# One matmul moved behind a block product in a gated graph network's step, and a score copy taken to where the scores are made

## The chip, the cores and the metric

The kernel runs on one core of a Trainium2 chip. The metric is the device time of one execution in microseconds (us), from the first to the last instruction of the program; the lower, the better. TensorE (PE in the profile, with its weight loads as PEld), VectorE (DVE), ScalarE (ACT), GpSimd (POOL) and SyncE (SP, DMA issues only) each run their own list of instructions in order, and wait for each other by semaphores.

## The reference, cut to what matters

The input is 64 graphs of 256 nodes with 256 features each (`x`, 64x256x256, float32) and an adjacency matrix per graph (`adj`, int32). Two layers follow each other, both with a layer norm and a relu ahead of them and a residual sum behind:

```python
# layer 0: three steps of a gated graph network (w_ih, w_hh are shared, weight[i] is the step's own)
h0 = relu(layernorm(x)); h = h0
for i in range(3):
    aggr = A^T @ (h @ weight[i])          # A = (adj != 0), per graph
    gi, gh = aggr @ w_ih.T + b_ih, h @ w_hh.T + b_hh
    r = sigmoid(gi_r + gh_r); z = sigmoid(gi_z + gh_z)
    n = tanh(gi_n + r * gh_n)
    h = (1 - z) * n + z * h
x = x + h
# layer 1: graph attention with 4 heads of 64
h = relu(layernorm(x)) @ W.T + b
logits = leaky_relu(l_src[i] + l_dst[j], 0.2), barred where adj is not 1
x = x + softmax(logits over j) @ h
```

`l_src` and `l_dst` are the two scores of each node and head, made from `h` and the vectors `a`.

## The kernel before, in words

**Tiling.** Graphs are taken in 32 pairs. The state of a pair lies transposed in one tile `hT_a` (128 partitions, two halves of the features, 2 x 256 nodes). `weight[i]` and `w_ih` are multiplied into one matrix `w_a` per step beforehand, so that a step multiplies the aggregated state `aggr` and the state `hT_a` by 256x256 weight blocks. For the r and z gates, and again for the state's part of n, the eight block products of a two-by-two block multiplication are brought down to seven by sums and differences of blocks (the tiles `T1` to `T4`, `T2n` to `T4n` and the weight blocks `S1` to `S4`, `NS1` to `NS4`); that is why partial results such as `m5`, `m5n`, `pd` and `pe` go from one bank of PSUM to another.

**Order.** The schedule is written out by hand. `plan` holds, for each tick, three lists: STEP (the gated step), READY (work for VectorE, ScalarE and GpSimd whose inputs are there) and REST (the rest, mainly TensorE work that fills in). The lists of a tick are issued in that order, and every engine runs what it was given in that order. A pair starts 18 ticks after the one before; a gated step takes six ticks (`tick_0` to `tick_5`) and a pair has three, at ticks 0, 12 and 24, so the steps of neighbouring pairs alternate and there is always exactly one step under way. The attention of a pair (values at ticks 37 and 38, score rows at 39, maxima, logits, exponentials, and the output products at 62 to 65) lies in the READY and REST lists of the ticks in which later pairs make their steps.

**Banks.** A step takes its banks of PSUM from a ring of five (`gate_bank`): `qa`, `qb`, `pc`, `p5` (called `p` in the profile), `pd`, `pe`, `pn0`, `pn1`. Everything else takes banks from a ring of three (`bank`).

**Around the change, first place.** `tick_0` makes n's first product (weight `N00`) in the left half of bank `qa`; ScalarE copies it to `qb` (L411). Then come the 16 aggregation matmuls in two banks `pa`, each copied to `aggr` by ScalarE (L422), and at the end the product `NS1` x `T1` in the right half of the same bank `qa`, which ScalarE copies to `m5n` (L424). `tick_1` began with n's second product (`N01`), accumulated onto the left half of `qa`; ScalarE turns that half into `hn` with the bias (`state_n`, L399). Then come `NS2` x `T2n` onto `qb`, a sum on VectorE (L433), the block product of the state for the r gate into `pc` (four matmuls in the program, eight in the profile), and the copy of `pc` to `pd` on ScalarE (L437). All matmuls of the step have float32 operands; the profile shows each as two. `part` (L396) issues the small products and `block` (L293) the block products.

**Second place.** `values` makes the four blocks of values and scores of a pair, two at tick 37 and two at tick 38: two matmuls for each into `pv`, and a sum with the bias on VectorE into `val` (L605). A row of `val` holds 4 x 65 values and then 8 scores. `score_rows`, at tick 39, copied the scores of all four blocks to a tile `score` (L636 on VectorE), and `as_rows` transposes it on TensorE (`pscore`, L615), copies the result out (L617) and sends it to DRAM, from where it is read back on all partitions. For the last pair the score rows are made per graph, at ticks 37 and 38.

Of the kernel before, what the change touches and what calls it, by code (L numbers as in the profile page):

```python
# [9 lines left out]
F32 = mybir.dt.float32  # L10
# [7 lines left out]
P = 128  # L18
# [8 lines left out]
def gated_gnn_then_gat_kernel(  # L27
# [39 lines left out]
    nc = tc.nc  # L67
    B, N, D = x.shape
    L = weight.shape[0]
    H, C2 = a.shape  # L70
# [5 lines left out]
    R = PB * KN  # L76
    T = PB * N
    VC = C + 1
    S0 = H * VC
# [7 lines left out]
    small = ctx.enter_context(tc.tile_pool(name="small", bufs=4))  # L87
# [9 lines left out]
    def bank(name):  # L97
        return ps_m.tile([P, 512], F32, tag="mm", name=name)
# [5 lines left out]
    def buf(tag, shape, name, dtype=F32):  # L104
        return sb.tile(shape, dtype, tag=tag, name=name, bufs=BUFS.get(tag, 1))
# [86 lines left out]
    N00, N01, N11, NS1, NS2, NS3, NS4 = range(7)  # L192
# [90 lines left out]
    def flat(y):  # L283
        return y.rearrange("q r d -> q (r d)")
# [4 lines left out]
    def block(pt, w, j, src, start=False):  # L289

        for c in range(KD):
            for k in range(KD):
                nc.tensor.matmul(  # L293
                    pt[:, ts(c, N)], w[:, k, j * D + c * P : j * D + (c + 1) * P], src[:, k, :],
                    start=start and c == 0 and k == 0, stop=(c == KD - 1 and k == KD - 1),
                    skip_group_check=True,
                )
# [64 lines left out]
    def of(y, i):  # L362
        return y[:, :, ts(i, N)]

    class Step:
# [60 lines left out]
        def tick_1(self):  # L426
            h0 = of(self.hT(), 0)
            q_a, q_b = self.qa, self.qb
            self.own("hn", [P, KD, T])
            self.part(q_a[:, :N], N01, h0[:, 1, :])  # L430
            self.state_n(0, 0, q_a[:, :N])
            self.part(q_b[:, :N], NS2, self.T2n)
            nc.vector.tensor_add(q_b[:, N:], q_b[:, :N], self.m5n)  # L433
            p_c = self.bank("pc")
            block(p_c, w_h, RH, h0, start=True)
            self.bank("p5")
            nc.scalar.copy(self.bank("pd"), p_c)  # L437
            T3 = self.own("T3", [P, KD, N])
            nc.vector.tensor_sub(T3, of(self.aggr, 1), of(self.hT(), 1))
            nc.vector.tensor_add(self.own("T2", [P, KD, N]), T3, h0)  # L440
# [64 lines left out]
    def plan_pair(p):  # L505
        t0 = APART * p
        v = {}
# [84 lines left out]
        blocks_of = {u: slice(u.start * KN, u.stop * KN) for u in units}  # L592

        def values(r0):
            def fn():
                if r0 == 0:
                    v["val"] = buf("val", [P, R, VW], f"val_{p}")
                for r in (r0, r0 + 1):
                    pt = bank(f"pv_{p}_{r}")
                    for k in range(KD):  # L600
                        nc.tensor.matmul(  # L601
                            pt[:, :VW], hb["hT"][:, k, ts(r, P)], w_val[:, k, :],
                            start=(k == 0), stop=(k == KD - 1),
                        )
                    nc.vector.tensor_add(v["val"][:, r, :], pt[:, :VW], b_val)  # L605
            return fn

        rest(37, values(0))
        rest(38, values(2))

        def as_rows(src, n, what, u):

            m = len(u) * KN * n
            pt = bank(f"p{what}_{p}_{u.start}")
            nc.tensor.transpose(pt[:m, :P], flat(src), ident)  # L615
            fl = buf("flat", [m, P], f"{what}_{p}_{u.start}")
            nc.vector.tensor_copy(fl, pt[:m, :P])  # L617
            rows = dram.tile([len(u), n, N], F32, tag=f"{what}{len(u)}", name=f"{what}_dram_{p}_{u.start}")
            for y in range(len(u)):
                for s in range(KN):  # L620
                    nc.sync.dma_start(rows[y, :, ts(s, P)], fl[(y * KN + s) * n : (y * KN + s + 1) * n, :])
            return {i: rows[i - u.start] for i in u}

        def on_all(rows, h0, blocks):

            src = rows[h0 : h0 + H, :]
            return bass.AP(tensor=src.tensor, offset=src.offset, ap=[[0, P], [0, blocks], [1, H * N]])

        scores, tops, drow, mrow, logits, link = {}, {}, {}, {}, {}, {}

        def score_rows(u):
            def fn():
                if u.start == 0:
                    v["score"] = small.tile([P, R, 2 * H], F32, tag="score", name=f"score_{p}", bufs=2)
                sc = v["score"][:, blocks_of[u], :]
                nc.vector.tensor_copy(sc, v["val"][:, blocks_of[u], S0:])  # L636
                scores.update(as_rows(sc, 2 * H, "score", u))
                for i in u:
                    drow[i] = buf("row", [P, H, N], f"drow_{p}_{i}")
                    nc.sync.dma_start(drow[i].rearrange("q h n -> q (h n)"), on_all(scores[i], H, 1)[:, 0, :])  # L640
            return fn
# [170 lines left out]
```

## Time and profile before

| | before |
|---|---|
| median time of three runs | 2687.61 us (2687.0 to 2689.67) |
| span of the profiled execution | 2687.4 us |
| TensorE matmuls busy | 2564.9 us (95%) |
| TensorE weight loads busy | 2259.6 us (84%) |
| VectorE busy | 1853.6 us (69%) |
| ScalarE busy | 1466.7 us (55%) |
| GpSimd busy | 653.4 us (24%) |
| DMA, mean | 89 GB/s |

Busy time is the union of an engine's instructions in the profile. Matmuls are pipelined, so that their spans overlap: one of the step's matmuls lasts 379 ns in the profile, while in an unbroken row one starts every 216 ns. A gap on TensorE is therefore read from the starts of matmuls. The work repeats for each pair: in the middle of the run the same matmul comes back every 79.9 us. In the profile's views a line such as "L396" is the line of the kernel's text, and names such as `qa<-T,w_n` say which tile is written from which.

### The profile page before, as it was taken

The page shows a single profiled execution, that of the slowest core. Times are in us where ns is not written, and L with a number is a line of the kernel's source. Part 1 is how long each engine was busy: PE and PEld are TensorE (multiplying, and loading weights), DVE is VectorE, ACT ScalarE, POOL GpSimd, SP SyncE. Part 2 cuts the span into 40 slices and gives each one's busy share as a digit, 9 for nine tenths or more (in the row PEclk, how much of TensorE's full clock was granted, in tenths as well). Part 3 has the DMA queues.
Part 4 walks back from the last instruction along what each step waited for, and adds up shares of the span by engine and source line. Part 5 has one row for each costly group of instructions (what it writes and reads, how often), then busy time and mean ns, then how long its engine had stood idle before and what let it go on. Part 6 is the DMA issues. An engine that isn't in the chain of part 4 may idle for free.

```text
span 2687.4 us, 38787 instructions
## 1 busy us (share of the span) xinstructions
PE 2564.9 (95%) x14074; PEld 2259.6 (84%) x14074; DVE 1853.6 (69%) x4497; ACT 1466.7 (55%) x3077; POOL 653.4 (24%) x518
## 2 busy tenths in 40 slices
PE   7899999999999999999999999999999999999985
PEld 5688888888888888888888888888888888888875
DVE  4567766777766777776677776677776677776663
ACT  2345555655555555655565555555555565555553
POOL 0012222222222222322222322222222222222221
PEclk9899999999999999999999999999999999999995
DMA  2004344434344433334443334443434443333444
GB/s 86 18 9 99 83 103 95 111 79 87 82 100 97 108 85 87 87 89 105 100 97 84 89 82 107 95 109 81 87 79 103 95 111 81 86 89 85 95 95 110
DMA packets 120320, 239.89 MB, mean 89 GB/s; under 512 B 9792, under 2 KB 79424, under 8 KB 120128
## 3 DMA queue, kind: packets, MB, share of 16 engines
q0 software_dynamic: 34272, 132.13, 25.6%
q1 hardware_dynamic: 80160, 102.52, 12.5%
q10 hardware_dynamic: 5696, 2.76, 0.4%
q8 instruction: 111, 1.82, 0.3%
q14 instruction: 81, 0.66, 0.1%
HBM read 219.82 MB, written 17.56 MB: 88 GB/s over the span
## 4 chain that ended last, share of the span: by engine, by line
PE 88%; ACT 5%; DVE 4%; issue 1%; DMA 1%; POOL 0%; ACTq 0%; SPq 0%; DVEq 0%; POOLq 0%
PE pd L293 18%; PE pn L293 12%; PE pc L293 10%; PE po L750 9%; PE qb L396 6%; PE p L293 6%; PE pe L293 6%; PE pa L418 5%; PE pv L601 4%; PE qa L396 4%; PE pback L552 3%; ACT aggr L422 2%; ACT zz L662 1%; PE pt_a L351 1%; PE pt_b L351 1%
## 5 line engine op out<-in xcount | busy, mean ns | idle before, releaser
L487 POOL TENSOR_TENSOR R<-hT_a,hn 128x512 f32<-128x512 f32 x192 | 318.3, 1658 | 930.4 <-ACT hn L484 865.9
L293 PE MATMUL pn<-aggr,w_a 128*128 128x256 f32 x1536 | 367.0, 382 | 0.0
L293 PE MATMUL pd<-T,w_a 128*128 128x256 f32 x1536 | 364.6, 380 | 0.0
L293 PEld LDWEIGHTS pn<-aggr,w_a 128*128 128x128 f32 x1536 | 287.1, 190 | 42.9 <-DVE pn L473 6.2
L293 PEld LDWEIGHTS pd<-T,w_a 128*128 128x128 f32 x1536 | 286.8, 190 | 36.9
L750 PEld LDWEIGHTS po<-val,zz 128*128 128x128 f32 x2048 | 258.6, 201 | 16.7 <-ACT zz L741 12.0
L750 PE MATMUL po<-val,zz 128*128 128x65 f32 x2048 | 255.9, 281 | 11.1 <-ACT zz L741 11.1
L690 DVE CUSTOM_DVE_ANT_0 any<-drow,noedge 128x256 f32<-128x256 f32 x512 | 244.7, 478 | 15.2 <-DMA drow<-score_dram 6.2
L763 POOL TENSOR_TENSOR x<-x,o 128x256 f32<-128x256 f32 x128 | 117.3, 917 | 524.4 <-DVE o L758 524.4
L403 ACT ACTIVATE R<-pc,brz 128x256 f32<-128x256 f32 x192 | 80.5, 470 | 296.6 <-PE pc L293 296.6
L484 ACT ACTIVATE hn<-pn,bi 128x256 f32<-128x256 f32 x384 | 160.4, 470 | 144.5 <-PE pn L293 144.4
L718 ACT ACTIVATE zz<-zz,val 128x256 f32<-128x256 f32 x512 | 231.9, 509 | 8.4 <-DMA zz<-score_dram 8.4
L502 DVE SCALAR_TENSOR_TENSOR R<-Z,R 128x512 f32<-128x512 f32 x192 | 131.7, 686 | 147.3 <-POOL R L487 142.6
L558 DVE TENSOR_TENSOR hNlo<-pback,hNhi 128x512 fp32r<-128x512 f32 x128 | 88.5, 691 | 183.0 <-ACT hNhi L557 183.0
L403 ACT ACTIVATE R<-pe,brz 128x256 f32<-128x256 f32 x192 | 80.5, 470 | 215.3 <-PE pe L293 215.3
L503 DVE SCALAR_TENSOR_TENSOR hT_a<-R,hn 128x512 f32<-128x512 f32 x192 | 174.9, 911 | 13.3
L473 DVE SCALAR_TENSOR_TENSOR pn<-R,hn 128x512 f32<-128x512 f32 x192 | 142.8, 744 | 59.8 <-ACT R L403 31.6
L293 PE MATMUL pd<-T,w_h 128*128 128x256 f32 x768 | 181.4, 379 | 0.0
L293 PE MATMUL pc<-hT_a,w_h 128*128 128x256 f32 x768 | 181.4, 379 | 0.0
L293 PE MATMUL p<-T,w_a 128*128 128x256 f32 x768 | 181.4, 379 | 0.0
L293 PE MATMUL pc<-aggr,w_a 128*128 128x256 f32 x768 | 181.4, 379 | 0.0
L293 PE MATMUL pe<-aggr,w_a 128*128 128x256 f32 x768 | 181.4, 379 | 0.0
(147 smaller groups left out, 5304.6 us busy)
## 6 DMA issues: line engine op xcount, KB each, us to landing
zz<-score_dram POOLq DMA_DIRECT2D x64, 1024.0 KB, 12.1
zz<-topT_dram POOLq DMA_DIRECT2D x62, 1024.0 KB, 8.0
adj<-in_adj_dram SPq DMA_DIRECT2D x64, 512.0 KB
drow<-score_dram SPq DMA_DIRECT2D x64, 512.0 KB
x<-in_x_dram SPq DMA_DIRECT2D x32, 512.0 KB
out_dram<-x SPq DMA_DIRECT2D x32, 512.0 KB
score_dram<-score SPq DMA_DIRECT2D x128, 4.0 KB
topT_dram<-topT SPq DMA_DIRECT2D x128, 2.0 KB
```

What stands on the lines that cost most here:

```text
L293: nc.tensor.matmul(pt[:, ts(c, N)], w[:, k, j * D + c * P : j * D + (c + 1) * P], src[:, k, :], start=start and c == 0 and k == 0, stop=(c ...
L396: nc.tensor.matmul(pt, w_n[:, j, :], src, start=start, stop=True, skip_group_check=True)
L403: nc.scalar.activation(of(dst, i)[:, c, :], src[:, c, :], AF.Tanh, bias=brz[:, g0 + c : g0 + c + 1], scale=0.5)
L418: nc.tensor.matmul(pt[:, ts(i, N)], hN[half][:, i * KN + s, ts(e, P)], edge[:, i * KN + s, :], start=(s == 0 and half == 0), stop=(s == KN ...
L473: nc.vector.scalar_tensor_tensor(by_c(self.bank(f"pn{i}")), of(self.R, i), 1.0, of(self.hn, i), op0=ALU.add, op1=ALU.mult)
L484: nc.scalar.activation(n__[:, c, :], p_n[:, c, :], AF.Tanh, bias=bi[:, 2 * KD + c : 2 * KD + c + 1])
L487: nc.gpsimd.tensor_sub(of(self.R, i), of(self.hT(), i), n__)
L502: nc.vector.scalar_tensor_tensor(d_, of(self.Z, i), 1.0, d_, op0=ALU.add, op1=ALU.mult)
L503: nc.vector.scalar_tensor_tensor(of(self.hT(), i), d_, 0.5, of(self.hn, i), op0=ALU.mult, op1=ALU.add)
L690: nc.vector.tensor_tensor_reduce(any_, drow[r // KN][:, h, :], v["noedge"][:, r, :], 1.0, -3.0e38, ALU.add, ALU.max, accum_out=v["top"][:, ...
L718: nc.scalar.activation(zz[:, h, :], zz[:, h, :], AF.Prelu, alpha=ALPHA, bias=v["val"][:, r, S0 + H + h : S0 + H + h + 1],)
L750: nc.tensor.matmul(po[:, ts(h_, VC)], logits[i][:, j, h_, ts(s, P)], v["val"][:, i * KN + j, ts(h_, VC)], start=(j == 0), stop=(j == KN - 1),)
```

## The change

In `tick_1` n's second product and the activation that reads it go behind the block product `pc`, with `NS2` x `T2n` on `qb` now first. The purpose is to put other matmuls between `NS1`, whose result ScalarE takes out of bank `qa`, and the next matmul that writes this bank. In the second place the copy of the scores goes from `score_rows` into `values`: each two blocks are copied right behind the sums that make them, so that the transpose at tick 39 finds its input ready. The arithmetic stays the same.

```diff
             self.own("hn", [P, KD, T])
-            self.part(q_a[:, :N], N01, h0[:, 1, :])
-            self.state_n(0, 0, q_a[:, :N])
             self.part(q_b[:, :N], NS2, self.T2n)
             nc.vector.tensor_add(q_b[:, N:], q_b[:, :N], self.m5n)
             p_c = self.bank("pc")
             block(p_c, w_h, RH, h0, start=True)
+            self.part(q_a[:, :N], N01, h0[:, 1, :])
+            self.state_n(0, 0, q_a[:, :N])
             self.bank("p5")
             nc.scalar.copy(self.bank("pd"), p_c)
...
                     nc.vector.tensor_add(v["val"][:, r, :], pt[:, :VW], b_val)
+                if r0 == 0:
+                    v["score"] = small.tile([P, R, 2 * H], F32, tag="score", name=f"score_{p}", bufs=2)
+                nc.vector.tensor_copy(v["score"][:, r0 : r0 + 2, :], v["val"][:, r0 : r0 + 2, S0:])
...
         def score_rows(u):
             def fn():
-                if u.start == 0:
-                    v["score"] = small.tile([P, R, 2 * H], F32, tag="score", name=f"score_{p}", bufs=2)
-                sc = v["score"][:, blocks_of[u], :]
-                nc.vector.tensor_copy(sc, v["val"][:, blocks_of[u], S0:])
-                scores.update(as_rows(sc, 2 * H, "score", u))
+                scores.update(as_rows(v["score"][:, blocks_of[u], :], 2 * H, "score", u))
```

## The prediction

> **What bounds the kernel now.** I read the page's busy times first, then the chain that ended last, then TensorE's list of waits, and last the timeline around each of the two largest waits. Busy times and chain, from the page:
>
> ```profile
> PE 2564.9 (95%) x14074; PEld 2259.6 (84%) x14074; DVE 1853.6 (69%) x4497; ACT 1466.7 (55%) x3077; POOL 653.4 (24%) x518
> ...
> PE 88%; ACT 5%; DVE 4%; issue 1%; DMA 1%; POOL 0%; ACTq 0%; SPq 0%; DVEq 0%; POOLq 0%
> ```
>
> TensorE sets the time: 88% of the chain are its own instructions, and no other engine is over 69% busy. What can be won without taking matmuls away is the 9% of ScalarE and VectorE in the chain, where TensorE stood still for them. Who they are is in the list of waits, once for the matmuls and once for the weight loads (total us, times, longest):
>
> ```profile
> PE qa L396 <- ACT m5n L424: 35.9, 66, 0.6
> PE pscore L615 <- DVE score L636: 18.8, 33, 2.0
> ...
> PEld qa L396 <- ACT m5n L424: 62.4, 66, 1.0
> PEld pscore L615 <- PE pc L293: 26.4, 30, 0.9
> ```
>
> The two largest waits are exactly the two that the diff touches. A matmul's span in the profile is longer than its share of an unbroken row, so the 35.9 and 18.8 us are lower ends of the loss; the idle time of the weight loads, 62.4 and 26.4 us, counts time too in which the matmul before still ran, and is an upper end. The true loss is read from starts. The timeline of one step (start, length, engine, line, names):
>
> ```profile
> 1191.79 0.59 PE L396 MATMUL qa<-T,w_n 128*128 128x256 f32 x2
> 1191.99 0.58 ACT L422 COPY aggr<-pa 128x512 f32<-128x512 f32 x1 [0.37 <-PE pa L418]
> 1192.47 0.38 ACT L424 COPY m5n<-qa 128x256 f32<-128x256 f32 x1
> ...
> 1192.91 0.70 PE L396 MATMUL qa<-hT_a,w_n 128*128 128x256 f32 x2 [0.52 <-ACT m5n L424]
> ...
> 1193.44 0.59 PE L396 MATMUL qb<-T2n,w_n 128*128 128x256 f32 x2
> ```
>
> In an unbroken row these matmuls start every 216 ns (the eight of `pc` take 1.73 us in the chain). Four of them lie between 1191.79 and 1193.44, which should take 0.86 us and took 1.65: 0.79 us lost. ScalarE copies the second half of `aggr` first and then `m5n`, and n's second product waits for that, though it writes the other half of the bank. In the next pair's step, in the chain of waits:
>
> ```profile
> 1242.19 0.99 ACT aggr L422 x2
> 1243.19 0.28 ACT m5n L424
> 1243.47 0.04 issue
> 1243.51 0.70 PE qa L396 x2
> ```
>
> There the `NS1` product started at 1242.27 and the product onto `qb` at 1244.05: 1.78 - 0.86 = 0.92 us lost. These two kinds of step alternate with a third, in which `pt_b` and `plink` already stand between the two products; that one has almost no wait (0.05 us), which is why the list says 66 times for 96 steps. For the scores:
>
> ```profile
> 1228.08 1.89 PE L293 MATMUL pc<-aggr,w_a 128*128 128x256 f32 x8
> 1228.28 0.70 DVE L457 TENSOR_TENSOR pe<-pd,m 128x512 f32<-128x512 f32 x1 [0.55 <-PE pd L293]
> ...
> 1230.15 0.17 DVE L636 COPY score<-val 128x32 f32<-128x32 f32 x1
> ...
> 1230.47 0.27 PE L615 MATMUL pscore<-ident,score 128*32 128x128 f32 x1 [0.51 <-DVE score L636]
> ```
>
> The eight `pc` matmuls end their row at 1228.08 + 1.73 = 1229.81; the transpose starts at 1230.47, 0.66 us later. The copy itself is short (0.17 us); it came late because VectorE first made `pe` and the three state sums `T`, `T3n` and `T2n`.
>
> **What the Trainium skill says.** "Perfetto Trace Analysis", section "Optimization Strategy", says to find the gaps of the engine that binds, see what semaphore ends each, and make that start sooner; that is the reading above. "TensorE: Matmul & The Clock Gate", section "Part 2: What happens when you issue a matmul", says that matmuls stay in program order while weight loads are pulled ahead of running matmuls. The trace agrees: a weight load of 190 ns costs nothing in the rows of `pc` (one start every 216 ns), but shows as 0.1 us behind each stop, 0.53 instead of 0.43 us from 1192.91 to 1193.44. So a matmul that waits holds all behind it, and moving independent ones ahead is the remedy. "VectorE: DVE Perf Modes", section "The TRN2 errata", says that small operations pay a fixed cost per instruction; here a score copy of 32 columns takes 173 ns and one of 16 (the last pair's) 174 ns, so halving a copy makes it no cheaper.
>
> **The change part by part.**
>
> *N's second product behind `pc`.* No instruction is added. Behind the `NS1` product now follow two matmuls on `qb` (0.43 us) and eight on `pc` (1.73 us) before bank `qa` is written again, 2.16 us in all. `m5n` was there 1.06 and 1.20 us after the start of `NS1`, the next writer now comes 2.59 us after it: over 1.3 us of room. What comes first now must not wait either. The product on `qb` needs `T2n` and the copy to `qb` (L411); in the slowest kind of step that copy ended at 1242.19, and the product will start at 1242.70. `pc` takes the bank that `pe` of the step before left, which ScalarE read long ago. So 0.79 and 0.92 us go, 0.85 on average: 66 x 0.85 = 56.1 us. The third kind I count at nothing, since behind the bf16 `plink` the 0.1 us of weight load stays.
>
> *The activation behind `pc`.* On ScalarE `hn` from `qa` (L399) now waits until about 3.0 us after `NS1` starts, and the copy `pd` (L437) queues behind it, together with an exponential (L741) in one kind of step and a leaky relu (L718) in the other. In the second kind of step: products end at 1245.29, `hn` (0.48) and `pd` (0.57) are done near 1246.5, before 1246.98 until now; the exponential (1.06) near 1247.6, needed by `po` at 1249.67 - 0.92 = 1248.75. `pd` is wanted by TensorE at 1251.41 - 0.92 = 1250.5. In the first kind `pd` is done near 1195.95 and wanted at 1198.7. Cost: nothing, hidden by matmuls.
>
> *VectorE, which doesn't all move up with TensorE.* In the first kind of step it works from 1191.98 to 1201.14 almost without a gap, so part of it keeps its old time. The sum on `qb` (L433) ended at 1194.62, and `NS3` onto `qb` will want it at 1196.04 - 0.79 = 1195.25: 0.63 us of room, the tightest place. `pe` (L457) had 0.36 us of idle time ahead of it and will lag TensorE by 0.79 - 0.36 = 0.43 us, where 1.63 us of room were. Behind it, `pn` (L473) had only 0.07 us of room; but it hangs on ScalarE's row from the end of `pc` (gate, `hNhi_a`, leaky relu, `hT_a`, `hn`), ahead of which ScalarE sat idle 2.46 us. That row moves up as a whole. Cost: nothing.
>
> *The score copies.* 31 pairs: one copy of 173 ns is replaced by two of about 174, in the ticks before, 31 instructions and 5.4 us of VectorE more. The second lies in the 0.55 us that VectorE sat idle ahead of `pe`. The transpose then finds its input over 1 us before it comes. 31 x 0.66 = 20.5 us. In the last pair the rows are made right behind the values, and nothing moves.
>
> Sum: 56.1 + 20.5 = 76.6 us, so 2687.6 - 76.6 = 2611 us. TensorE's clock was granted in full (1.00) through the middle of the run and can't rise; stops of under 1 us were not costing clock.
>
> **The rivals.**
>
> *Half comes back as new waits.* For it: VectorE and ScalarE keep their old times in part of each step, and 0.63 us is little. Against it: every other place has over 0.8 us. If `NS3` or `po` waits 0.6 us in 66 steps, 39.6 us are lost: about 2651.
>
> *Another chain paces the step.* If the chain from `pn` through ScalarE, GpSimd and the state's update back to the next product were binding, the 56 us would come back whole and only the scores' 20.5 remain: 2667. Against it: TensorE waits for `hT_a` only twice (3.4 us in its list).
>
> *Slower.* If `pn`, with its 0.07 us, slipped by the length of the moved activation and the copy behind it (0.48 + 0.57 us) in all 96 steps, that is 101 us, over the 76.6 won: 2712. For it: in-order ScalarE. Against it: the 2.46 us of idle time between the moved work and that row.
>
> **How the numbers follow.** The forecast, 0.82; half back, 0.09; paced elsewhere, 0.05; slower, 0.03; a remainder of 0.01 for no change. Together: faster 0.96, within 0.2% 0.01, slower 0.03. Low end: the upper ends of the loss, 62.4 + 26.4 = 88.8 us, give 2599. High end: the lower ends, 35.9 + 18.8 = 54.7 us, give 2633; I put it at 2636, which holds the forecast with a few us of new waits.
>
> **What would show it.** In the changed profile: no row of `qa` waiting for `m5n`, none of `pscore` waiting for `score`; a pair's period of 79.9 - 0.79 - 0.92 - 0.66 = 77.5 us; ScalarE's and VectorE's share of the chain down from 9% to some 6%; VectorE's busy time up by about 5 us. Wrong would be a new row on TensorE of tens of us, above all `qb` for its sum, `pd` or `pn` for VectorE, or `po` for `zz`.

## The result, and the profile after

The changed kernel takes 2612.04 us (median; 2610.02 to 2613.19), the kernel before 2688.64 us in the same session: a ratio of 0.9714, 95% interval 0.9698 to 0.9731. That is 76.6 us less, where 2611 us had been forecast. Busy times and the chain that ended last, from the page of the kernel after:

```profile
PE 2539.7 (97%) x14074; PEld 2266.0 (87%) x14074; DVE 1849.2 (71%) x4528; ACT 1462.2 (56%) x3077; POOL 653.0 (25%) x518
...
PE 95%; DVE 2%; DMA 1%; issue 1%; ACT 0%; POOL 0%; ACTq 0%; POOLq 0%; SPq 0%; DVEq 0%
```

TensorE's own work has gone from 88% to 95% of the chain, ScalarE's from 5% to nothing, VectorE's from 4% to 2%. TensorE's list of waits (total us, times, longest) now begins with what happens once, at the start or in the last pair:

```profile
PE ptopT L618 <- DVE top L701: 13.1, 3, 5.8
PE po L749 <- ACT zz L740: 11.6, 4, 8.3
PE pwa L262 <- DMA a_exp<-in_L_gnn_a_dram: 8.3, 2, 6.3
...
PE pscore L618 <- DVE score L608: 2.4, 3, 0.8
```

The row for `qa` and `m5n` is gone, and of the 33 waits of `pscore` the three of the last two pairs are left. The timeline of the step that answers to the first one shown of before:

```profile
1235.87 0.59 PE L396 MATMUL qa<-T,w_n 128*128 128x256 f32 x2
1236.30 0.59 PE L396 MATMUL qb<-T2n,w_n 128*128 128x256 f32 x2
1236.55 0.38 ACT L424 COPY m5n<-qa 128x256 f32<-128x256 f32 x1
1236.73 1.89 PE L293 MATMUL pc<-hT_a,w_h 128*128 128x256 f32 x8
...
1238.26 0.43 DVE L431 TENSOR_TENSOR qb<-qb,m5n 128x256 f32<-128x256 f32 x1
1238.46 0.59 PE L396 MATMUL qa<-hT_a,w_n 128*128 128x256 f32 x2
...
1239.14 0.47 ACT L399 ACTIVATE hn<-qa,bhn 128x256 f32<-128x256 f32 x1 [1.41 <-PE qa L396]
...
1239.33 0.60 PE L396 MATMUL qb<-T3n,w_n 128*128 128x256 f32 x2
```

The starts 1235.87, 1236.30, 1236.73 and 1238.46 are those of an unbroken row (two matmuls in 0.43 us, eight in 1.73). `m5n` is out of the bank at 1236.93, and its next writer comes at 1238.46, 1.53 us later. The price of the move is visible on ScalarE: it sits idle for 1.41 us until the product is there, and nothing on TensorE waits for that. The score transpose, in the timeline of another pair:

```profile
1348.46 0.17 DVE L608 COPY score<-val 128x16 f32<-128x16 f32 x1
1348.78 1.89 PE L293 MATMUL pc<-aggr,w_a 128*128 128x256 f32 x8
1348.98 0.70 DVE L457 TENSOR_TENSOR pe<-pd,m 128x512 f32<-128x512 f32 x1 [0.34 <-PE pd L293]
...
1350.50 0.27 PE L618 MATMUL pscore<-ident,score 128*32 128x128 f32 x1
```

The second half of the scores is copied ahead of `pe`, in time in which VectorE had nothing to do. The transpose starts at 1350.50, and the row of `pc` ends at 1348.78 + 1.73 = 1350.51: no gap. In 30 of the 32 pairs the gap was 0.67 us before and is nothing now.

One pair's period, from an NS1 product to the same one of the next pair, is 77.50 us, after 79.9. The table by windows of that stretch has TensorE busy for the whole of it:

```profile
1235.87:1313.37 77.50, 77.50 (x438) 69.50 (x437) 56.84 (x140) 45.52 (x96) 20.62 (x16) 1.00 0.42 96
```

(The columns are the window's length, then busy time and instructions of TensorE's matmuls, its weight loads, VectorE, ScalarE and GpSimd, then TensorE's clock, the DMA share and GB/s.)

### The profile page after: what moved, and what is told of

It reads as the page before. It is cut to its first block, busy times and chain, and to the rows that moved or that the text cites. A ratio compares the mean times of both kernels' runs of the same rounds, so it can differ in the third digit from the quotient of the medians.

```text
span 2610.4 us, 38818 instructions
## 1 busy us (share of the span) xinstructions
PE 2539.7 (97%) x14074; PEld 2266.0 (87%) x14074; DVE 1849.2 (71%) x4528; ACT 1462.2 (56%) x3077; POOL 653.0 (25%) x518
## 4 chain that ended last, share of the span: by engine, by line
PE 95%; DVE 2%; DMA 1%; issue 1%; ACT 0%; POOL 0%; ACTq 0%; POOLq 0%; SPq 0%; DVEq 0%
PE pd L293 19%; PE pn L293 13%; PE pc L293 13%; PE po L749 9%; PE pa L418 7%; PE qb L396 6%; PE pe L293 6%; PE p L293 6%; PE qa L396 5%; PE pv L601 4%; PE pback L552 3%; PE pt_a L351 1%; PE pt_b L351 1%; PE plink L652 1%; PE pc L220 0%
## 5 line engine op out<-in xcount | busy, mean ns | idle before, releaser
L749 PE MATMUL po<-val,zz 128*128 128x65 f32 x2048 | 255.9, 281 | 11.6 <-ACT zz L740 11.6
```

Of the source, the lines that this page charges most:

```text
L749: nc.tensor.matmul(po[:, ts(h_, VC)], logits[i][:, j, h_, ts(s, P)], v["val"][:, i * KN + j, ts(h_, VC)], start=(j == 0), stop=(j == KN - 1),)
```

## The experiments

The theory was that each of the two waits is a loss of its own, that the first one is the lateness of the copy out of bank `qa` and nothing else, and that VectorE's sum on `qb`, which `NS3` waits for, is the nearest limit. (NS1, NS3 and so on stand for the products with these weight blocks; the three kinds of step are those of the prediction.) Rivals: the parts share one gain, the order of ScalarE's work is what counted, or VectorE's work counts in full.

**One part alone.** The first run moves n's second product and leaves the scores:

```diff
-            self.part(q_a[:, :N], N01, h0[:, 1, :])
-            self.state_n(0, 0, q_a[:, :N])
...
             block(p_c, w_h, RH, h0, start=True)
+            self.part(q_a[:, :N], N01, h0[:, 1, :])
+            self.state_n(0, 0, q_a[:, :N])
```

> Only n's second product and its activation are moved behind the block product; the scores are copied where they were. If the two waits are separate losses of TensorE, this part brings 66 x 0.85 = 56 us: about 2632 us, and the wait of the score transpose stays (18.8 us in the list). If the parts share their gain (the row of work from one wait to the next is paced by something else), it brings clearly less than 56 us, under 45: over 2643 us.

The second makes the score copies in `values`, takes the copy out of `score_rows` as the change does, and leaves the product where it was:

```diff
                     nc.vector.tensor_add(v["val"][:, r, :], pt[:, :VW], b_val)
+                if r0 == 0:
+                    v["score"] = small.tile([P, R, 2 * H], F32, tag="score", name=f"score_{p}", bufs=2)
+                nc.vector.tensor_copy(v["score"][:, r0 : r0 + 2, :], v["val"][:, r0 : r0 + 2, S0:])
...
```

> Only the score copies are made with the values; n's second product stays ahead. Separate losses: 31 x 0.66 = 20.5 us less, about 2668 us, with TensorE's wait for m5n unchanged (35.9 us, 66 times). If the transpose then waits for something else that was hidden behind the copy, nothing comes: 2688 us.

Measured: 2633.22 us with the move alone (ratio 0.9792, 0.9776 to 0.9809) and 2668.68 us with the scores alone (0.9923, 0.9908 to 0.9937), against 2689.18 us before. That is 56.0 and 20.5 us, and 76.5 us together, as much as both at once. The list of waits keeps in each run exactly the row that was not treated. Move alone:

```profile
PE pscore L615 <- DVE score L636: 18.8, 33, 2.0
```

Scores alone:

```profile
PE qa L396 <- ACT m5n L424: 35.9, 66, 0.6
```

The two losses are separate, and both sizes read from starts hold. The same two rows would have given 35.9 and 18.8 us by the matmuls, 62.4 and 26.4 by the weight loads.

**Less cover.** N's second product directly behind the one on `qb`, so that 0.43 us of other work lies between NS1 and the next writer in place of 2.16:

```diff
             self.part(q_b[:, :N], NS2, self.T2n)
+            self.part(q_a[:, :N], N01, h0[:, 1, :])
+            self.state_n(0, 0, q_a[:, :N])
             nc.vector.tensor_add(q_b[:, N:], q_b[:, :N], self.m5n)
             p_c = self.bank("pc")
             block(p_c, w_h, RH, h0, start=True)
-            self.part(q_a[:, :N], N01, h0[:, 1, :])
-            self.state_n(0, 0, q_a[:, :N])
```

> As the changed kernel, but n's second product follows directly behind the product on qb, ahead of the block product: 0.43 us of other matmuls stand between NS1 and the next writer of its bank in place of 2.16 us. If the loss is the time that the copy m5n is late, 0.43 of the 0.85 us are covered in each of 66 steps and 0.42 us stay: 2612 + 28 = about 2640 us, TensorE again waiting for m5n 66 times. If what helped was any other matmul in between, or the later activation on ScalarE, it is all (2612 us) or none (2668 us).

Measured: 2635.95 us (0.9804, 0.9789 to 0.9818), 24 us over the changed kernel's 2612. The gain goes with the cover, neither all nor none. In the first kind of step the second product now starts 1.11 us behind NS1 where 0.86 would be unbroken, and its second half 0.10 us late: 0.35 us; in the second kind it is 0.41. Times 66, at a mean of 0.38, that is 25 us; 0.42 and 28 us had been expected.

This run is worth a look for how it reads. TensorE's list of matmul waits has no row for `qa` and `m5n` at all, though 24 us are lost there. The list of weight loads and the chain of waits show it; first the list:

```profile
PEld qa L396 <- ACT m5n L424: 33.9, 66, 0.5
```

and the chain in one step:

```profile
1245.79 0.59 ACT aggr L422
1246.37 0.28 ACT m5n L424
1246.66 0.04 issue
1246.70 0.70 PE qa L396 x2
```

A span of 379 ns in a row that starts one every 216 ns covers the first 163 ns of any stop. Of a stop of 0.25 to 0.30 us some 0.1 us is left to see, and the list has no row for it.

**Another remedy for the same wait.** N's second product and its activation stay first in `tick_1`, as before; NS1 goes up front in `tick_0`, and its copy ahead of those of `aggr`:

```diff
             self.part(q_a[:, :N], N00, h0[:, 0, :], start=True)
+            self.part(q_a[:, N:], NS1, self.T1[:, 0, :])
             nc.scalar.copy(q_b[:, :N], q_a[:, :N])
+            nc.scalar.copy(self.own("m5n", [P, N]), q_a[:, N:])
...
-            self.part(q_a[:, N:], NS1, self.T1[:, 0, :])
-            nc.scalar.copy(self.own("m5n", [P, N]), q_a[:, N:])
```

> The score copies as in the changed kernel. In the step n's second product and its activation stay where they were in the kernel before; in place of moving them, the NS1 product goes up front, directly behind n's first product, and ScalarE copies m5n ahead of aggr. Now sixteen aggregation matmuls (1.92 us) stand between NS1 and the next writer. If the wait for the copy out of the bank is the whole cause, this is worth the same as the move: about 2612 us, 2608 to 2616. If the gain came from the order of ScalarE's work (the activation behind the block product), only the score part is left: 2668 us.

Measured: 2613.77 us (0.9718, 0.9704 to 0.9733), the same as the move. The order of ScalarE's activation is not the cause; what counts is that the bank's reader is done when its next writer comes. One pair's period is even a little shorter, 77.42 to 77.44 us, but a wait appeared at the start of the program:

```profile
PE qa L396 <- DVE T L384: 4.7, 2, 2.6
```

In the first two steps of the first pair NS1 up front came before VectorE had made `T1`. So one more run kept NS1 at the end of the tick in these two steps (`early` is true in all others), beside the changed kernel once more on the same chip:

```diff
-            self.part(q_a[:, N:], NS1, self.T1[:, 0, :])
+            early = self.n_ not in ("0_0", "0_1")
+            if early:
+                self.part(q_a[:, N:], NS1, self.T1[:, 0, :])
             nc.scalar.copy(q_b[:, :N], q_a[:, :N])
-            nc.scalar.copy(self.own("m5n", [P, N]), q_a[:, N:])
+            if early:
+                nc.scalar.copy(self.own("m5n", [P, N]), q_a[:, N:])
...
                 nc.scalar.copy(aggr[:, e, :], pt)
+            if not early:
+                self.part(q_a[:, N:], NS1, self.T1[:, 0, :])
+                nc.scalar.copy(self.own("m5n", [P, N]), q_a[:, N:])
```

> The changed kernel as it is, on the same chip as the next one: 2612 us, 0.971 of the kernel before.

> NS1 up front as in the run before, but in the first two steps of the first pair, where no other pair's work covers VectorE's sums and NS1 up front waited 2.2 and 2.6 us for T1, the product stays at the end of the tick. That gives these 4.8 us back: about 2609 us, 0.970 of the kernel before, some 3 us under the changed kernel, which the intervals may not separate. If the wait comes back elsewhere at the start, it stays at 2614 us.

Measured: 2612.69 us for the changed kernel (0.9711, 0.9698 to 0.9724) and 2610.26 us for this one (0.9701, 0.9687 to 0.9714). Its median is the lowest of all, by 2.4 us. The periods fit that (2 us less from the sixth step to the last but one), and its five runs (up to 2610.82) lie below the four beside them (from 2612.18). But the intervals of the ratios overlap, and one of the changed kernel's first four runs took 2610.02, so a gain of 0.1% over the changed kernel is not settled.

**How near the next limit is.** The changed kernel with two, and with four, more subtractions on VectorE in each step, right ahead of its sum on `qb`:

```diff
             self.part(q_b[:, :N], NS2, self.T2n)
+            for _ in range(2):
+                nc.vector.tensor_sub(of(self.hn, 0)[:, 1, :], self.T2n, h0[:, 1, :])
             nc.vector.tensor_add(q_b[:, N:], q_b[:, :N], self.m5n)
```

> The changed kernel with two more subtractions of 128x256 on VectorE in each step, right ahead of its sum on qb (they write a part of hn that ScalarE fills later; the output is the same). In an unbroken row such a subtraction takes 0.335 us, so 0.67 us more ahead of the sum. The room in front of NS3 was 0.64 us in the tightest kind of step (32 of 96), less about 0.1 us for the semaphore, and 1.6 and 3.3 us in the others: about 0.13 us of wait in 32 steps, 4 us in all, about 2616 us (2612 to 2620). If VectorE's work in the step counts in full, 96 x 0.67 = 64 us more: 2676 us.

> The same with four subtractions, 1.34 us. If NS3 in the tightest kind of step is the place: 1.34 - 0.54 = 0.80 us in 32 steps, 26 us, about 2638 us (2630 to 2646), with a row of TensorE waiting for qb from VectorE 30 or so times; the other kinds still have room. If the delay slips on from there to pn or to the next step, it is more: over 2650 us. If other work of VectorE has more slack than I read, under 2625 us.

Measured: 2621.13 us with two (0.9744, 0.973 to 0.9757) and 2662.67 us with four (0.9895, 0.9882 to 0.9909): 8.4 and 50 us more than the changed kernel of the same session, both over what was expected, though far from counting in full. The place is the one named. With four, TensorE's list of waits has this row, and the timeline of a step of the first kind follows:

```profile
PE qb L396 <- DVE qb L433: 29.3, 33, 1.0
```

```profile
1259.67 1.80 DVE L432 TENSOR_TENSOR hn<-T2n,hT_a 128x256 f32<-128x256 f32 x4
...
1261.38 0.42 DVE L433 TENSOR_TENSOR qb<-qb,m5n 128x256 f32<-128x256 f32 x1
...
1261.86 0.70 PE L396 MATMUL qb<-T3n,w_n 128*128 128x256 f32 x2 [0.97 <-DVE qb L433]
```

The size of the added work was mis-set: the four put the sum off by 1261.38 - 1259.67 = 1.71 us, where 4 x 0.335 = 1.34 had been assumed. They write the same tile one after the other, and in the trace each waits for the one before, by a semaphore: 0.458 us from start to start. Only the sum, which has no such wait for the last of them, follows in 0.343. With 1.71 us the step of the first kind lengthened by 1.22 us (24.80 against 23.58 from one `pc` to the next) and that of the second by 0.40; 31 x 1.62 = 50 us, all of what was measured. So the room is 1.71 - 1.22 = 0.49 us in the first kind, where 0.54 had been expected. It is the 0.64 us less two things that the lines above show: the sum ends 0.06 us before `NS3` starts, and the second half of `NS3` comes 0.10 us late, so that its span is 0.70 us in place of 0.60. In the second kind the first of them waits too, for the instruction ahead of it, which makes 4 x 0.458 = 1.83 us, and the room is 1.83 - 0.40 = 1.43 us, from 1.60. Two subtractions, 0.343 + 0.458 = 0.80 us, should then cost 0.31 in 31 steps, 9.6 us, against 8.4 measured; from one `pc` to the next that run does lose 0.31 us in the first kind and nothing in the others. Nothing slipped on to `pn` or the next step, which the expectation had named as the reason for a time over 2650: the weight loads' wait for `pn` is 6.3 us here too, and from `pc` of the third kind to that of the second it is 25.43 us, as without the added work.

## Why the prediction was right, step by step

*TensorE bounds the kernel, and the two waits are plain losses.* Shown: the parts add up (56.0 + 20.5 against 76.6 us), TensorE is busy over a whole period, and the clock in the middle stayed at 1.00. That the forecast and the measured gain agree to 0.1 us is luck, as the interval of the ratio is some 9 us wide.

*56.1 us from n's second product.* Shown, 56.0; but two terms were off and, by luck, made up for each other. The second kind of step won 0.84 us, not 0.92, read from one `pc` to the next: 0.08 of the 0.92 was the late second half of the NS1 product itself (0.30 us behind its first half in place of 0.22), which the change leaves. The timeline of after shows where it comes from:

```profile
1284.34 0.38 ACT L411 COPY qb<-qa 128x256 f32<-128x256 f32 x1
...
1284.77 0.30 PEld L396 LDWEIGHTS qa<-T,w_n 128*128 128x128 f32 x2
1284.79 0.68 PE L396 MATMUL qa<-T,w_n 128*128 128x256 f32 x2
```

NS1 too writes a bank whose other half ScalarE is reading, and its weight load starts only as that copy ends, at 1284.72. It is a small case of the same wait, and leaves no gap between NS1 and the matmul ahead of it. The run with NS1 up front, ahead of that copy, has no such delay. The third kind, counted at nothing, won 0.10 us per step: its wait of 0.05 us, and half of the 0.10 us of weight load behind `plink` that was expected to stay (the second half of the product there came 0.32 us behind the first, and comes 0.27 behind it now). That is 66 x 0.81 + 30 x 0.10 = 56.5 us by the sum of the kinds.

*20.5 us from the scores.* Shown, 20.5, with no new wait of the transpose.

*The activation behind `pc` costs nothing.* Shown as far as time goes: `hn` starts 3.27 us after NS1 in the first kind of step (about 3.0 was worked out), ScalarE idles 1.41 us ahead of it, and no matmul came to wait for what is queued behind: `pd` has no row, and `po` waits for `zz` 4 times as before, 11.6 us in place of 11.1.

*VectorE lags, with 0.63 us of room ahead of NS3.* Shown: in the step at 1235.87, in the first timeline above, the sum ends 1239.33 - 1238.69 = 0.64 us ahead of NS3, and the cost of the added work in both runs fits a room of 0.49 us there.

*The rivals.* Half back or another pace: the period fell by 2.39 us against 2.37 forecast, so nothing came back. By the starts it is 0.78 and 0.84 of the first two kinds, 0.10 of the third and 0.67 of the scores. Slower: `pn` kept its small room; the weight loads' wait for it, 6.2 us before, is 6.3 after.

*The share of the chain* was a wrong sign: ScalarE's and VectorE's 9% were to go down to some 6% and went down to 2%. They had been read as time in which TensorE stood still, but the chain follows the waits back over work that TensorE ran beside. In the second kind of step, as the prediction shows it, ScalarE's two pieces ahead of n's second product are 0.99 + 0.28 = 1.27 us, where 0.92 were lost. The forecast did not rest on this share.

*VectorE's busy time* was to rise by about 5 us and fell from 1853.6 to 1849.2. The copies did add their share (33 of 173 ns became 64 of 175 ns, 5.7 to 11.2 us). But busy time is a union, and with less waiting VectorE's spans overlap more: added one by one they come to 2063.9 us before and 2073.8 after.

## What to carry to other kernels

Where one engine is busy nearly all the time, list its waits, take each one's size from the starts of its instructions against their unbroken pace, and look for independent work to put into the gap, or for a way to issue the awaited producer earlier; both were worth the same here. A matmul can wait for the reader of a bank of PSUM even where it writes the other half. The runs don't show whether the chip needs this wait or only the program's semaphores make it; two separate banks for the two halves were not tried. The cure needs other work for as long as the reader is late: here 0.43 us of it took away half of the loss, 1.92 and 2.16 us all of it, and nothing in between was tried. Before moving work, write down the room at each place that keeps its old time: 0.63 us read from the trace turned out to be 0.49 us in use, mostly because a stop, once it is there, makes the second half of the matmul late as well.

## What the runs showed of the hardware that had not been expected

A chain of VectorE instructions that write the same tile, each waiting for the one before, ran at 0.458 us per 128x256 subtraction; the sum behind the last of them, without such a wait, followed in 0.343 us.

A stop of TensorE of 0.25 to 0.30 us left no row in the list of matmul waits and cost, with the 0.10 us of the late second half, 24 us over 66 steps; it was visible only in the weight loads, the chain and the starts.
